# A four-layer scan network on one core: order of the y copy, of the z and C stores, of a job's first loads, and PSUM banks at the end

## The chip, the cores and the metric

The kernel runs on one core of one Trainium2 chip. The metric is the device time of one execution in microseconds. The runs shown are three executions of the kernel before, and one profiled execution, whose trace all views come from.

## What is computed

The input is 4 images of 64 x 64 positions with 96 channels. Four layers follow one another, each a mixer with a residual and a small feed-forward net with a residual. Cut to what matters here, in layers 1 to 3:

```python
# x: (4, 64, 64, 96); layers 1..3
xz = layernorm(x) @ in_proj_w.T                 # 192 channels for x, 192 for z
xc = silu(depthwise_conv3x3(x_part) + conv_b)
# four directions: rows, columns, and both reversed; 16 states
dA = exp(dt * A);  h = dA * h + (dt * u) * B;  y = sum_n h_n * C_n + D * u
y  = sum of the four directions, layernorm, * silu(z), @ out_proj_w.T
x  = x + y
t  = x + W2 @ relu(W1 @ layernorm(x) + b1) + b2     # operands rounded to fp8, sums to fp16
```

Layer 0 has another recurrence (A, B and C are projections of each position, the output is gated), and the same feed-forward net.

## The kernel before, in words

The work is one program, written out in order for each engine: a wrapper (`InOrder`) makes every engine carry out its instructions in the order in which the Python code emits them. All instructions bear the line of that wrapper (L78) in the profile, so the views go by tile names.

**Stages.** `gated` does layer 0 for all images. Then `scans` does 12 stages (layers 1 to 3, four images each). A stage has 24 items: 2 directions, 4 segments of T = 1024 positions, 3 chunks of 128 partitions (64 channels in two orders). An item has NS = 16 steps, one for each state n. So there are 12 x 24 x 16 = 4608 steps k.

**One step k of `scans`**, in the order of emission: ACT copies the end of the last scan (`carry(k - 1)`); SP issues the rows of C for step k + 2, two broadcast loads into one of six tiles `c`, and ACT makes the decays `da` for k + 2 (`c_rows`, `decays`); PE broadcasts B for k + 1 into one of two wide PSUM tiles `bc` (`b_rows`); POOL multiplies the last state row by C (`times_c(k - 1)`, h in three tiles); if step k - 4 was an item's last, `store` copies the sum `acc` from PSUM into `y` on ACT and sends it to HBM with four DMAs; DVE multiplies du by B and scans (`scan(k, beside)`), and between those two `beside` emits side work; PE adds the product of step k - 3 into `acc` (`accumulate`, two PSUM banks, one buffer). The first `accumulate` of an item also puts in D * u or the y of the other direction. `store` of an item is thus emitted at n = 3 of the next one, just before the first `accumulate` of that item, which needs the same `acc`.

**Side work.** Side work is in generators; each `yield` ends a link, and `pump` emits one link. A generator that yields True needs a free bank among two single PSUM banks (`bank`, `release`, `settle`). `prepare_chunk` makes delta and du for the next item, `prepare_segment` projects u to dt, B and C rows of the next segment and sends C to HBM (`cs`), from where `c_rows` broadcasts it. Both get one link a step, and are drained at n = 13.

**Jobs.** `between(im, layer, dst)` is the end of one layer and the start of the next for one image: `first` loads y (two halves of `cols_a` and two of `part_c`, and the first strip's `pad` tiles); then, over 8 strips of 512 positions, three chains side by side: `joins` (y of four directions transposed and added on PE, `y_t`), `mixers` (norm, gate by z, `out_proj`), `feeds` (the feed-forward net). Then `takes` (norm, input projection, z) and `convolves` (3 x 3 convolution, Silu, u and z to HBM). `Job.step` gives its chains `rate` rounds of links a step: 1.65 for the next stage's image, 2.6 for the last ends of images 0 to 2 in the last two stages and for layer 0's. A norm needs a logarithm on ACT; norms wait in `pending`, and `logarithms` serves all at once: at n = 11 of each item, in `prepare_chunk`, or when a job has waited `patience` rounds. The job of the next stage must be done at n = 4 of item 22 of a stage; what is left then is emitted at once.

**The end.** The last image's end runs alone after the scans: `Job(between(images[-1], 3, images[-1].dst), patience=1).finish()`. There logarithms come when no chain can emit a link.

**PSUM.** One pool `pbc` holds the two wide tiles (four banks) and the two single banks; a second pool (`pl0`, then `pac`) holds the sums (two banks).

The lines that the steps are about:

```python
            if 0 <= k - 1 <= last:
                carry(k - 1)
            if k + 2 <= last:
                c_rows(k + 2)
                decays(k + 2)
...
            if k >= 4 and (k - 4) % NS == NS - 1:
                store(items[(k - 4) // NS])
            if k <= last:
                scan(k, beside)
            if 0 <= k - 3 <= last:
                accumulate(k - 3)
            settle()
```

Of the kernel before, what the change touches and what calls it, by code (L numbers as in the profile page):

```python
# [10 lines left out]
F32 = mybir.dt.float32  # L11
# [88 lines left out]
def metaformer(ctx: ExitStack, tc: tile.TileContext, x, l0_ab, l0_rest, ssm, ffn, out):  # L100
# [13 lines left out]
    def const(name, shape, dtype=F32):  # L114
        return pools[1].tile(shape, dtype, name=name)

    def wide():
        return pbc.tile([128, T], F32, tag="bc", name="bc")


    banks = {"free": 2, "back": 0}

    def bank(name):
        banks["free"] -= 1
        return pbc.tile([128, MM], F32, tag="ps", name=name)

    def release():
        banks["back"] += 1

    def settle():  # L130
        banks["free"] += banks["back"]
        banks["back"] = 0
# [423 lines left out]

    def gate_z(im, s, hold):
        if s < NSTRIP:
            t = slice(s * MM, (s + 1) * MM)
            for z, a in zip(hold["z"].pop(s), (0, 128)):  # L560
                act.activation(z, z, AF.Silu)
                sp.dma_start(out=im.z[a : a + z.shape[0], t], in_=z)

    def convolve(im, layer, s, hold):

        lo, hi = hold["pads"].pop(s)
        taps = weights[layer]
        w = taps.w
        raw = []
        groups = (  # L570
            [(taps.lo[:, t, :], lo[:, t // 3 : t // 3 + SR, t % 3 : t % 3 + HW]) for t in range(9)],
            [(taps.hi[:, t, :], hi[:, 0:SR, t : t + HW]) for t in range(3)]
            + [(taps.hi[0:64, 3 + t, :], hi[0:64, 2 : 2 + SR, t : t + HW]) for t in range(3)],
        )
        for i, group in enumerate(groups):
            ps = bank("conv")
            for at, (lhs, rhs) in enumerate(group):
                pe.matmul(ps, lhs, rhs, start=at == 0, stop=at == len(group) - 1)
                yield
            v = sb(1, f"u{i}", [128, MM])  # L580
            act.copy(v, ps)
            release()
            yield i == 0
            raw.append(v)
        for i, v in enumerate(raw):
            act.activation(v, v, AF.Silu, bias=w[:, W_CB + i : W_CB + i + 1])
        gate_z(im, s + 1, hold)
        yield
        yield
        t = slice(s * MM, (s + 1) * MM)  # L590
        cols_a, part_c = hold["cols"]
        sp.dma_start(out=im.u[0, 0:64, t], in_=raw[0][0:64])
        sp.dma_start(out=im.u[1, 0:64, t], in_=raw[0][64:128])
        sp.dma_start(out=im.u[2, 0:64, t], in_=raw[1][0:64])
        for p, src, dst, c0, nc_ in (
            (slice(0, 128), raw[0], cols_a, 0, HW),
            (slice(0, 64), raw[1], part_c, 0, HW // 2),
            (slice(64, 128), raw[1], part_c, HW // 2, HW // 2),
        ):
            pool.tensor_copy(  # L600
                dst[p].rearrange("p (c r) -> p r c", r=HW)[:, SR * s : SR * s + SR, :],
                src[p].rearrange("p (r c) -> p r c", c=HW)[:, :, c0 : c0 + nc_],
            )
            if p.start or p.stop == 128:
                yield
        if s == NSTRIP - 1:
            yield
            sp.dma_start(out=im.u[1, 64:128, :], in_=cols_a[0:64])
            sp.dma_start(out=im.u[0, 64:128, :], in_=cols_a[64:128])
            for k in range(2):  # L610
                sp.dma_start(
                    out=im.u[2, 64:128, k * L // 2 : (k + 1) * L // 2],
                    in_=part_c[64 * k : 64 * k + 64],
                )

    def between(im, layer, dst=None):
# [8 lines left out]
        def first():  # L625
            if layer:
                cols_a, part_c = hold["cols"] = columns()
                sp.dma_start(out=cols_a[0:64], in_=im.y[1, 64:128, :])
                sp.dma_start(out=cols_a[64:128], in_=im.y[0, 64:128, :])
                for k in range(2):  # L630
                    sp.dma_start(
                        out=part_c[64 * k : 64 * k + 64],
                        in_=im.y[2, 64:128, k * L // 2 : (k + 1) * L // 2],
                    )
                load_y(im, 0, hold)
            yield
            yield
            yield

        yield [Chain(first())]  # L640
        done = {"y": 0, "x": 0, "end": 0}
# [55 lines left out]
        def convolves():  # L697
            yield lambda: done["in"] > 0
            gate_z(im, 0, hold)
            for s in range(NSTRIP):  # L700
                yield lambda: done["in"] > min(s + 1, NSTRIP - 1)
                yield True
                yield from convolve(im, layer + 1, s, hold)
                done["out"] += 1
# [3 lines left out]
    class Job:  # L708
# [23 lines left out]
                    logarithms()  # L732
                    self.waited = 0

        def finish(self):
            while not self.done:
                self.step()
                settle()


# [22 lines left out]
    def prepare_segment(item, sg):  # L763

        xp = weights[item.layer].xp
        m = NB3 + 2 * R

        def project(ps, a, b, k):

            for c in range(3):  # L770
                o = (3 * item.d + c) * XPW
                cols = slice(k * MM, (k + 1) * MM)
                pe.matmul(
                    ps[0 : b - a],
                    xp[:, o + a : o + b],
                    sg.us[c][:, cols],
                    start=c == 0,
                    stop=c == 2,
                )
                if c:  # L780
                    yield

        sg.rows = sb(1, "rows", [128, T])
        for k in range(2):
            cols = slice(k * MM, (k + 1) * MM)
            ps = bank("x_proj_b")
            yield from project(ps, 0, m, k)

            bs = sg.bs[:, cols]
            act.copy(sg.rows[NB3:m, cols], ps[NB3:m])  # L790
            sg.steps = k == 1
            act.copy(bs, ps[0:NB3])
            yield
            rem = sg.rows[0:NB3, cols]
            dve.tensor_tensor(rem, ps[0:NB3], bs, ALU.subtract)
            release()
            yield
            for p in (32, 64):
                act.copy(bs[p : p + 32], rem[p : p + 32])
            yield k == 0  # L800
        pool.tensor_tensor(sg.bs[64:96], sg.rows[64:96], sg.bs[64:96], ALU.subtract)
        for k in range(2):
            cols = slice(k * MM, (k + 1) * MM)
            yield True
            ps = bank("x_proj_c")
            yield from project(ps, m, m + NC2, k)
            act.copy(sg.rows[0:NC2, cols], ps[0:NC2])
            release()
        sp.dma_start(out=sg.cs, in_=sg.rows[0:NC2])

    def prepare_chunk(item):
# [48 lines left out]
    def scans(stages, jobs, pac):  # L860
# [94 lines left out]
        def accumulate(k):  # L955
# [7 lines left out]
                    add_quarters(i, i.yf, stacked, True, False)  # L963
            add_quarters(i, h, stacked, False, n == NS - 1)

        def store(i):
            y = sb(2, "y", [128, T])
            act.copy(y, i.acc)
            for j in range(2):
                for k in range(2):  # L970
                    o = 64 * (j ^ k)
                    t = i.seg * T + k * MM
                    sp.dma_start(
                        out=i.im.y[i.chunk, 64 * j : 64 * j + 64, t : t + MM],
                        in_=y[o : o + 64, j * MM : (j + 1) * MM],
                    )

        chain = segment = None
# [15 lines left out]
        for k in range(last + 5):  # L994
# [23 lines left out]
            def beside():  # L1018
# [5 lines left out]
                        drain(segment, work)  # L1024
                work()

            if 0 <= k - 1 <= last:
                carry(k - 1)
            if k + 2 <= last:
# [5 lines left out]
                b_rows(k + 1)  # L1035
            if 0 <= k - 1 <= last:
                times_c(k - 1)
            if k >= 4 and (k - 4) % NS == NS - 1:
                store(items[(k - 4) // NS])
            if k <= last:  # L1040
                scan(k, beside)
            if 0 <= k - 3 <= last:
                accumulate(k - 3)
            settle()
# [241 lines left out]
    for i, im in enumerate(images):  # L1286
        im.src = x[i * L : (i + 1) * L, :]
        im.dst = out[i * L : (i + 1) * L, :]
    with tc.tile_pool(name="pl0", bufs=1, space=bass.MemoryType.PSUM) as pl0:
        gated(images, Job(between(images[0], 0), 2.6, patience=1), pl0)  # L1290
    stages = [(im, layer) for layer in range(1, 4) for im in images]
    jobs = []
    for at in range(len(stages)):
        jobs.append([])
        if at + 1 < len(stages):
            im, layer = stages[at + 1]
            jobs[-1].append(Job(between(im, layer - 1), 1.65))

        for im in {10: images[:2], 11: images[2:3]}.get(at, ()):
            jobs[-1].append(Job(between(im, 3, im.dst), 2.6))  # L1300
    with tc.tile_pool(name="pac", bufs=1, space=bass.MemoryType.PSUM) as pac:
        scans(stages, jobs, pac)
    Job(between(images[-1], 3, images[-1].dst), patience=1).finish()

# [115 lines left out]
```

## Time and profile before

| what | value |
|---|---|
| median of three runs | 19681.59 us (19680.81 to 19689.28) |
| the profiled execution | 19688.32 us, span 19686.5 us |
| layer 0 (`gated`) | 0 to 1817 us |
| scans of 12 stages | 1817 to 19394 us, 4608 steps |
| the last image's end | 19394 to 19687 us |
| mean granted clock of PE | 0.815 |
| a scan, a multiply on DVE | 2343 ns, 1208 ns |
| copy of y on ACT | 288 times, median 993 ns |
| C rows, from issue to landing | median 4.2 us |

In the page and the answers, DVE is VectorE, ACT ScalarE, POOL GpSimd, PE TensorE's matmuls, PEld its weight loads, SP SyncE, which issues the DMAs here. A group line reads: engine, operation, out<-in, shapes, count | busy us, mean ns of one | idle time of the engine just before these instructions, and what ended most of it. A waits line reads: who <- for whom: us in total, times, longest. A timeline line reads: start us, length us, engine, line, operation, tiles, shapes, count, and in brackets the idle time before and what ended it.

### The profile page before, as it was taken

To read this page: it belongs to the slowest core of one execution; us is meant where nothing else is said; L and a number is where in the kernel's file an instruction comes from. 1 tells how busy PE (TensorE), PEld (TensorE's weight loads), DVE (VectorE), ACT (ScalarE), POOL (GpSimd) and SP (SyncE) were. 2 spreads that over 40 slices of the span, in tenths; PEclk is the share of its full clock that TensorE was granted. 3 is DMA by queue.
4 is the path that set the end of the run, shared out by engine and by line. 5 is a ranking of instruction groups with operands and counts; after the bars stand their busy time and mean duration, and the time that the engine had idled before them with its cause. 6 is when DMAs were issued, how large, how long until landed. Compare 5 with 4: busy or idle time off the path is not lost. (4 is left out here: it accounts for less than half of the span.)

```text
span 19686.5 us, 224801 instructions
## 1 busy us (share of the span) xinstructions
PE 16267.7 (83%) x70400; PEld 4750.9 (24%) x70400; DVE 17666.9 (90%) x13768; ACT 12256.8 (62%) x19331; POOL 15495.8 (79%) x10086
## 2 busy tenths in 40 slices
PE   8998787787888887787887888787888888888876
PEld 3332121121122222222222222222222222222223
DVE  6757999999999999999999999999999999998884
ACT  4544665665665665665666666666666666666664
POOL 3435888888888888888888888888888888878884
PEclk9998787787887797797797787797887787787886
DMA  2213676666676667666666676666666666676663
GB/s 52 50 48 87 169 185 168 170 187 164 171 189 173 166 184 182 168 185 178 170 188 176 170 186 172 170 188 174 171 186 172 170 189 174 171 187 169 165 176 89
DMA packets 1269876, 3192.65 MB, mean 162 GB/s; under 512 B 440336, under 2 KB 440560, under 8 KB 1262544
## 3 DMA queue, kind: packets, MB, share of 16 engines
q1 hardware_dynamic: 1268688, 3178.27, 61.5%
q8 instruction: 568, 9.31, 0.2%
q14 instruction: 620, 5.08, 0.1%
HBM read 2818.81 MB, written 308.28 MB: 159 GB/s over the span
## 5 line engine op out<-in xcount | busy, mean ns | idle before, releaser
L78 POOL TENSOR_TENSOR c<-h,c 128x1024 f32<-128x1024 f32 (+1 forms) x4992 | 11334.8, 2277 | 3377.8 <-DVE h L78 1478.0
L78 DVE TENSOR_TENSOR_SCAN h<-da,carry,bc 128x1024 f32<-128x1024 f32 x4608 | 10795.4, 2343 | 530.3 <-POOL c L78 17.0
L78 PE MATMUL acc<-c,twice 64*64 64x512 f32 x36864 | 6215.7, 751 | 20.1 <-POOL c L78 20.0
L78 ACT ACTIVATE da<-delta,decay 128x1024 f32<-128x1024 f32 x4608 | 5280.9, 1147 | 1491.5 <-DVE h L78 1475.6
L78 DVE TENSOR_TENSOR bc<-du,bc 128x1024 f32<-128x1024 f32 x4608 | 5565.6, 1208 | 488.4 <-PE bc L78 461.6
L78 PE MATMUL bc<-bs,sel 96*128 96x512 bf16 x9216 | 3384.4, 455 | 2343.3 <-DVE h L78 2235.9
L78 ACT COPY carry<-h 128x1 f32<-128x1 f32 x3456 | 649.5, 188 | 3374.5 <-DVE h L78 3368.7
L78 PEld LDWEIGHTS <-sel 96*128 96x128 bf16 x9216 | 552.2, 101 | 7301.0 <-DVE h L78 5519.2
L78 PEld LDWEIGHTS acc<-c,twice 64*64 64x64 f32 x36864 | 1130.7, 153 | 2799.4 <-issue 1860.2
L78 ACT ACT_TABLE_LOAD x1155 | 1481.9, 1283 | 36.5 <-DVE mv L78 20.3
L78 PE MATMUL conv<-pad,tap_lo 128*128 128x512 f32 x1728 | 906.5, 634 | 0.0
L78 PE MATMUL dt_proj<-rows,w 12*128 12x512 f32 x1152 | 826.5, 804 | 6.4 <-ACT delta L78 6.4
L78 ACT ACTIVATE du<-e,ones 128x1024 f32<-128x1024 f32 x576 | 659.3, 1145 | 199.3 <-POOL delta L78 194.5
L78 POOL TENSOR_TENSOR delta<-delta,du 128x1024 f32<-128x1024 f32 x288 | 679.8, 2361 | 72.0 <-ACT du L78 70.3
L78 PE MATMUL x_proj_b<-u,xp 128*108 128x512 f32 x1152 | 687.6, 713 | 46.4 <-DMA xp<-in_ssm 15.5
L78 PE MATMUL x_proj_c<-u,xp 128*32 128x512 f32 x1152 | 642.0, 672 | 76.1 <-ACT rows L78 67.0
L78 POOL TENSOR_TENSOR e<-e,du 128x1024 f32<-128x1024 f32 x288 | 679.8, 2360 | 2.4 <-ACT du L78 2.4
L78 ACT ACTIVATE c<-c,l_bias 128x512 f32<-128x512 f32 x384 | 263.6, 686 | 670.5 <-PE c L78 665.9
L78 POOL TENSOR_TENSOR du<-delta,u 128x1024 f32<-128x1024 f32 x288 | 680.4, 2363 | 0.1
L78 POOL TENSOR_TENSOR delta<-delta,e 128x1024 f32<-128x1024 f32 x288 | 678.8, 2357 | 0.1
L78 PE MATMUL conv<-pad,tap_hi 128*128 128x512 f32 (+1 forms) x1152 | 601.8, 624 | 0.6 <-ACT u L78 0.5
L78 DVE TENSOR_TENSOR_SCAN h<-da,l_carry,bc 128x512 f32<-128x512 f32 x384 | 491.4, 1280 | 41.9 <-DVE bc L78 2.3
(152 smaller groups left out, 15200.8 us busy)
## 6 DMA issues: line engine op xcount, KB each, us to landing
c<-cs SPq DMA_DIRECT2D x9216, 256.0 KB, 4.2
u<-u SPq DMA_DIRECT2D x288, 512.0 KB, 6.7
y<-y SPq DMA_DIRECT2D x1152, 128.0 KB, 3.2
y<-y SPq DMA_DIRECT2D x144, 512.0 KB, 6.8
xr<-x SPq DMA_DIRECT2D x224, 192.0 KB, 5.1
u<-u SPq DMA_DIRECT2D x288, 128.0 KB, 3.6
pad<-y SPq DMA_DIRECT2D x288, 128.0 KB, 4.9
z<-zl SPq DMA_DIRECT2D x96, 256.0 KB, 2.0
```

The lines of the kernel that those rows point to most:

```text
L78: ins = f(*a, **k).ins
```

## The change

Four edits, and a regrouping of PSUM pools that the last one needs.

1. `store` is parted. `take` (the copy of `acc` into `y`) is emitted first in the step, ahead of `carry` and `decays`; the four DMAs are emitted after `scan`.
2. The stores of z go into `store_z`, two links after the Silu that makes z. The store of C in `prepare_segment` goes one link after its last copy.
3. `first` yields nine times instead of three when the layer has a scan before it (layer > 0), so that it takes ten links.
4. The wide tiles go into a pool of their own (`pbig`), which is closed with `pac` before the last image's end; that end then takes its banks from a pool of six (`pend`). Its job has rate 3 instead of 1.4, and `finish(eager=True)` calls `logarithms` after each round in which a norm is pending.

```diff
+    wides = []
+
     def wide():
-        return pbc.tile([128, T], F32, tag="bc", name="bc")
+        return wides[0].tile([128, T], F32, tag="bc", name="bc")
...
-    banks = {"free": 2, "back": 0}
+    banks = {"free": 2, "back": 0, "pool": pbc}
     def bank(name):
         banks["free"] -= 1
-        return pbc.tile([128, MM], F32, tag="ps", name=name)
+        return banks["pool"].tile([128, MM], F32, tag="ps", name=name)
...
     def gate_z(im, s, hold):
         if s < NSTRIP:
+            for z in hold["z"][s]:
+                act.activation(z, z, AF.Silu)
+
+    def store_z(im, s, hold):
+        if s < NSTRIP:
             t = slice(s * MM, (s + 1) * MM)
             for z, a in zip(hold["z"].pop(s), (0, 128)):
-                act.activation(z, z, AF.Silu)
                 sp.dma_start(out=im.z[a : a + z.shape[0], t], in_=z)
...
         gate_z(im, s + 1, hold)
         yield
         yield
+        store_z(im, s + 1, hold)
         t = slice(s * MM, (s + 1) * MM)
         cols_a, part_c = hold["cols"]
         sp.dma_start(out=im.u[0, 0:64, t], in_=raw[0][0:64])
...
                 load_y(im, 0, hold)
-            yield
-            yield
-            yield
+            for _ in range(9 if layer else 3):
+                yield
...
             gate_z(im, 0, hold)
+            yield
+            yield
+            store_z(im, 0, hold)
             for s in range(NSTRIP):
...
-        def finish(self):
+        def finish(self, eager=False):
+
             while not self.done:
                 self.step()
+                if eager and pending:
+                    logarithms()
                 settle()
...
             act.copy(sg.rows[0:NC2, cols], ps[0:NC2])
             release()
+        yield
         sp.dma_start(out=sg.cs, in_=sg.rows[0:NC2])
...
+        def take(i):
+            i.y = sb(2, "y", [128, T])
+            act.copy(i.y, i.acc)
+
         def store(i):
-            y = sb(2, "y", [128, T])
-            act.copy(y, i.acc)
             for j in range(2):
                 for k in range(2):
                     o = 64 * (j ^ k)
                     t = i.seg * T + k * MM
                     sp.dma_start(
                         out=i.im.y[i.chunk, 64 * j : 64 * j + 64, t : t + MM],
-                        in_=y[o : o + 64, j * MM : (j + 1) * MM],
+                        in_=i.y[o : o + 64, j * MM : (j + 1) * MM],
                     )
...
+            full = items[(k - 4) // NS] if k >= 4 and (k - 4) % NS == NS - 1 else None
+            if full is not None:
+                take(full)
             if 0 <= k - 1 <= last:
                 carry(k - 1)
...
-            if k >= 4 and (k - 4) % NS == NS - 1:
-                store(items[(k - 4) // NS])
             if k <= last:
                 scan(k, beside)
+            if full is not None:
+                store(full)
...
+    with tc.tile_pool(name="pbig", bufs=2, space=bass.MemoryType.PSUM) as wides_pool:
+        wides.append(wides_pool)
...
-    Job(between(images[-1], 3, images[-1].dst), patience=1).finish()
+    with tc.tile_pool(name="pend", bufs=6, space=bass.MemoryType.PSUM) as pend:
+        banks.update(free=6, back=0, pool=pend)
+        Job(between(images[-1], 3, images[-1].dst), 3, patience=1).finish(eager=True)
```

More of the change, by code (lines that the diff above doesn't have):

```diff
@@ L1288, in metaformer @@
         im.dst = out[i * L : (i + 1) * L, :]
[L1289 to L1302, printed above, removed]
-    Job(between(images[-1], 3, images[-1].dst), patience=1).finish()
+    with tc.tile_pool(name="pbig", bufs=2, space=bass.MemoryType.PSUM) as wides_pool:
+        wides.append(wides_pool)
+        with tc.tile_pool(name="pl0", bufs=1, space=bass.MemoryType.PSUM) as pl0:
+            gated(images, Job(between(images[0], 0), 2.6, patience=1), pl0)
+        stages = [(im, layer) for layer in range(1, 4) for im in images]
+        jobs = []
+        for at in range(len(stages)):
+            jobs.append([])
+            if at + 1 < len(stages):
+                im, layer = stages[at + 1]
+                jobs[-1].append(Job(between(im, layer - 1), 1.65))
+            for im in {10: images[:2], 11: images[2:3]}.get(at, ()):
+                jobs[-1].append(Job(between(im, 3, im.dst), 2.6))
+        with tc.tile_pool(name="pac", bufs=1, space=bass.MemoryType.PSUM) as pac:
+            scans(stages, jobs, pac)
+    with tc.tile_pool(name="pend", bufs=6, space=bass.MemoryType.PSUM) as pend:
+        banks.update(free=6, back=0, pool=pend)
+        Job(between(images[-1], 3, images[-1].dst), 3, patience=1).finish(eager=True)
 def _layer0(W_in, b_in, W_out, b_out, gamma, beta):
```

## The prediction

> **What bounds the kernel now.** I read the busy shares first, then busy times by stretch, then the table of waits, then the timeline around the places that the change touches.
>
> ```profile
> PE 16267.7 (83%) x70400; PEld 4750.9 (24%) x70400; DVE 17666.9 (90%) x13768; ACT 12256.8 (62%) x19331; POOL 15495.8 (79%) x10086
> L78 DVE TENSOR_TENSOR_SCAN h<-da,carry,bc 128x1024 f32<-128x1024 f32 x4608 | 10795.4, 2343 | 530.3 <-POOL c L78 17.0
> L78 DVE TENSOR_TENSOR bc<-du,bc 128x1024 f32<-128x1024 f32 x4608 | 5565.6, 1208 | 488.4 <-PE bc L78 461.6
> ```
>
> VectorE (DVE) is the bound. 4608 steps of one multiply (1208 ns) and one scan (2343 ns) make 16.4 of the 19.7 ms; the only large wait is for the broadcast of B by TensorE (PE), 461.6 us. The next view gives busy time in the scan stages, in the first joins of the last image's end, and in that whole end (columns: window, length, then PE, PEld, DVE, ACT, POOL busy, granted clock, DMA share, GB/s).
>
> ```profile
> 1817.00:19394.00 17577.00, 14493.68 (x65366) 4019.14 (x65366) 16465.77 (x11920) 11330.46 (x17389) 14733.86 (x8758) 0.81 0.67 176
> 19421.00:19442.00 21.00, 19.20 (x128) 12.85 (x128) 3.04 (x16) 2.60 (x8) 0.00 (x0) 0.50 0.46 104
> 19394.00:19687.00 293.00, 176.47 (x864) 109.15 (x864) 30.22 (x144) 104.03 (x227) 67.02 (x137) 0.50 0.19 45
> ```
>
> DVE idles 17577 - 16466 = 1111 us in the scans[...]. So all four edits together fight over some 600 us in the scans and over the 293 us tail, in which no engine is full.
>
> ```profile
> DVE bc L78 <- PE bc L78: 461.6, 271, 20.7
> POOL c L78 <- DMA c<-cs: 285.7, 78, 14.0
> ACT y L78 <- PE acc L78: 164.4, 87, 13.9
> PE acc L78 <- ACT y L78: 163.7, 154, 2.9
> PE y_t L78 <- DMA pad<-y: 116.5, 12, 23.3
> SPq L78 <- ACT zl L78: 332.5, 96, 27.7
> ```
>
> Columns: total, times, longest. The copy of y holds PE for 163.7 us, and PE holds that copy for as long. A job's first loads hold PE 12 times, one of them in the tail. The z stores hold the queue of SyncE (SP) for 332.5 us.
>
> [...] C rows land in 4.2 us by the page's median, yet POOL waits 10 to 14 us for one behind a job's first loads. [...] 19.2 of 21 us busy, clock still 0.50. I count on no faster clock there.
>
> **Step 1, y first on ACT (288 copies of 993 ns).** Now the copy stands behind carry (188 ns) and decays (1147 ns), both of which wait for the last scan; in the new order it stands ahead of them. Two copies as they are now:
>
> ```profile
> 10489.10 0.99 ACT L78 COPY y<-acc 128x1024 f32<-128x1024 f32 x1
> 10490.15 1.09 PE L78 MATMUL acc<-u,skipd 64*64 64x512 f32 x8 [1.56 <-ACT y L78]
> ...
> 12015.09 1.01 ACT L78 COPY y<-acc 128x1024 f32<-128x1024 f32 x1 [1.45 <-PE acc L78]
> ```
>
> In the first, PE waits for the copy, and an earlier copy helps. In the second the copy waits for PE, and nothing is won. Over 287 copies in the timeline (the last has no next chunk) I took the time at which the sum is complete, A, against the end of the scan that carry waits for, E. A is before E in 89; there the copy could start sooner, all cases together 213 us. Capped by PE's wait after the same copy that is 126 us, and capped again by DVE's wait for B in the three steps after it, 29 us (46 without PE's cap). I take 35 us won. In the other 198 A is after E. Now carry and decays run while PE finishes; in the new order they wait too, so ACT ends the step later by A - E, at most 0.19 + 1.15 = 1.34 us: 194 ACT-us in all. Queued behind are decays, the delta activations that free PE's banks, and the job's copies. Decays of step k+2 have cover: they are due at E + 2 x 3.60 + 1.25 = 8.45 us and would end at A + 2.3; A - E is 4.1 us at the ninth decile and 6.8 at most. The rest reaches DVE through PE only in part; the trace doesn't show the share. Between 0 and 194 us I take a tenth, 20 us, since ACT is busy 64% of this stretch. Net -15 us, bounds -46 and +148. The four y stores go to SP after the scan's helpers instead of before; nobody reads them soon, so zero.
>
> **Step 2, z and C sent behind their data.** 96 pairs of z stores go two links later, 96 C stores one link. I looked behind every z wait over 4 us in the scans: in the 15 us after it no POOL wait for C rows follows. C rows are issued two steps ahead into six buffers, which is the cover; the longest hold there is 6.4 us. In layer 0 the next strip's x load does come late (DVE waits of 5 us in seven strips), but the u stores ahead of it need Silu results that are ready only half a microsecond sooner, and they stay ahead. So 0 us; at best about 7 x 5 = 35 us. The extra link of C is drained before the next chunk needs it. Loss: a job gets 8 links more (six of step 3), 8/1.65 x 3.6 = 17 us later; jobs end at least 8 steps (29 us) ahead of the forced drain, so zero.
>
> **Step 3, ten links for first loads.** Six links more: at 1.65 a step 6/1.65 x 3.60 = 13.1 us later for y_t on PE, at 2.6 a step 8.3 us. Eleven jobs in the scans load y (columns: start, length):
>
> ```profile
> 10499.72 0.77 PE L78 MATMUL y_t<-ident,pad 128*128 128x128 f32 x2 [5.87 <-DMA pad<-y]
> 10502.07 4.67 POOL L78 TENSOR_TENSOR c<-h,c 128x1024 f32<-128x1024 f32 x2 [11.67 <-DMA c<-cs]
> 10505.04 1.23 DVE L78 TENSOR_TENSOR bc<-du,bc 128x1024 f32<-128x1024 f32 x1 [6.31 <-PE bc L78]
> ```
>
> Eight look like this, with PE waits of 3.8 to 6.2 us, so 13.1 us removes them, and DVE waits of 6.0, 5.0, 5.7, 6.3, 4.7, 5.1, 5.4 and 5.4 = 43.6 us. **But POOL is late next.** Its C row still lands where it does, and h has three buffers, so the third scan after must wait for POOL. A place without any y_t shows that wait alone:
>
> ```profile
> 2918.10 2.34 POOL L78 TENSOR_TENSOR c<-h,c 128x1024 f32<-128x1024 f32 x1 [8.81 <-DMA c<-cs]
> 2920.47 2.35 DVE L78 TENSOR_TENSOR_SCAN h<-da,carry,bc 128x1024 f32<-128x1024 f32 x1 [1.76 <-POOL c L78]
> ```
>
> For the example: scan at 10489.18 + 3 x 3.604 = 10499.99, POOL done at 10502.07 + 2.35 = 10504.42, so 4.4 us stay. Over the eight this way 27.5 us stay, and with 0.5 us of disturbance each 31.5: 12 us won. The other three run at 2.6 a step, with PE waits of 23.3, 13.4 and 15.6 us and DVE waits of 20.7, 11.3 and 14.4. Here 8.3 us go from each, 25 us; the rest stays. Step 3: -37 us, bounds -12 and -60.
>
> **Step 4, the tail on six banks.** 27 us until the first pads land, then PE works 174.8 us in 266, 21.8 us a strip, and the chain shows out_proj returning every 60 us for two strips. Logarithms come only when all chains stand still, so feeds, mixers and joins go in convoys. With eager logarithms and banks for each, they overlap, and PE's 21.8 us a strip are the floor. Each norm costs two table loads of 1.28 us (ten loads now, up to 32 after: 28 us more on ACT, under PE). I take 25 us a strip: 27 + 16 (first join 11, logarithm to refinement 5) + 8 x 25 + 22 (last feed) = 265, so -28 us. At 22 a strip -52, at 29 it is +4. PSUM pools and their changeover: nothing, one wait for finished work.
>
> **Sum.** -15 + 0 - 37 - 28 = -80 us. The profiled execution took 19688.3 us (span 19686.5, 1.8 around it); it becomes 19608. It lies 6.7 us over the median of the runs, so I forecast 19681.6 - 80 = **19602 us**, 0.41% less. A difference under 0.2% (39 us) can't be told from no change.
>
> **Rivals.** *The covers are thin* (chance 0.17): 46 us at the copies, 58 at the loads, 52 in the tail, 156 us in all, 19526. For it: PE waits for y in 154 places. Against: POOL's wait stands behind the loads. *The next wait takes over* (0.16): nothing net at the copies, 12 us at the loads since POOL and PE still wait, 10 in the tail: -22, 19660. For it: POOL waits 285.7 us for C rows, which no edit removes. *ACT's head of line* (0.12), the slower side: the copy at the queue's head waits for PE in 198 places, and all 194 us come through to DVE. -35 + 194 - 37 - 28 = +94, 19776. It decides against the change from 51% of the 194 us on (100 us undone), by over 0.2% from 72%. For it: ACT releases the banks that PE needs at n = 4 and 5, where DVE's steps run over 3.60 us by 80 and 116 us in all, more than at any other n. Against it: PE, late by itself, leaves ACT idle time there.
>
> **Chances.** The forecast case (-40 to -125) has 0.55. Faster by over 0.2%: 0.55 + 0.17 = 0.72; within: 0.16; slower: 0.12. The range goes from 19530 to 19672; it leaves out the slower rival and the far end of the first, under 0.2.
>
> **What would show it.** PE's wait for ACT's y falls below 60 us and ACT's wait for PE's sum rises; the DVE waits at the eight first loads shrink to 3 to 5 us with POOL's C as releaser; PE's wait for pads is left in the tail and the three late jobs; POOL's 286 us for C rows stay; the tail is 240 to 280 us with 20 to 32 table loads. I am wrong if DVE's waits for PE grow after the copies, or if the later jobs meet the u loads at new places and the scans lose there what the loads gave.

## The result, and the profile after

The changed kernel took 19613.61 us in the median of six runs (19604.67 to 19656.49), the kernel before 19682.17 us in runs on the same chip: a ratio of 0.9968 with a 95% interval of 0.9957 to 0.9978, or -63 us (-85 to -43). The forecast of 19602 us lies 12 us below it. The profiled execution took 19605.71 us, with a span of 19603.9 us. The total came out as forecast. Two of its four parts did not, and the experiments are about that.

The page's two groups of DVE, which are to be held against the first block of the prediction:

```profile
L78 DVE TENSOR_TENSOR_SCAN h<-da,carry,bc 128x1024 f32<-128x1024 f32 x4608 | 10797.5, 2343 | 598.7 <-POOL c L78 80.8
L78 DVE TENSOR_TENSOR bc<-du,bc 128x1024 f32<-128x1024 f32 x4608 | 5567.1, 1208 | 417.8 <-PE bc L78 389.6
```

Busy times are within 2 us of those of before, means the same. DVE's idle time ahead of the multiplies fell from 488.4 to 417.8 us, that ahead of the scans rose from 530.3 to 598.7 us, and POOL's C is now named for 80.8 us where it was 17.0. One wait has taken the place of another. Busy times in the scans and in the last image's end:

```profile
1804.00:19388.00 17584.00, 14533.33 (x65366) 4017.53 (x65366) 16467.88 (x11919) 11313.07 (x17391) 14733.80 (x8758) 0.81 0.67 175
19388.00:19604.00 216.00, 162.97 (x864) 108.75 (x864) 29.75 (x144) 113.57 (x235) 67.51 (x137) 0.51 0.26 61
```

The scans took 17584 us, no less than the 17577 us of before. The end fell from 293 to 216 us. The waits:

```profile
ACT y L78 <- PE acc L78: 708.9, 246, 14.2
DVE bc L78 <- PE bc L78: 389.6, 271, 5.1
POOL c L78 <- DMA c<-cs: 295.3, 80, 13.6
DVE h L78 <- POOL c L78: 81.5, 37, 12.5
PE y_t L78 <- DMA pad<-y: 42.2, 4, 23.2
PE acc L78 <- ACT y L78: 35.4, 69, 2.1
```

PE's wait for the copy fell from 163.7 to 35.4 us. The copy's own wait for PE rose from 164.4 to 708.9 us: ACT now stands with the copy at its head, in 246 places where it was 87. POOL's wait for C rows is about what it was (285.7 before).

A job's first loads, at the place that the prediction shows:

```profile
10508.51 4.65 POOL L78 TENSOR_TENSOR c<-h,c 128x1024 f32<-128x1024 f32 x2 [10.51 <-DMA c<-cs]
10510.89 2.35 DVE L78 TENSOR_TENSOR_SCAN h<-da,carry,bc 128x1024 f32<-128x1024 f32 x1 [3.46 <-POOL c L78]
10514.12 0.63 PE L78 MATMUL y_t<-ident,pad 128*128 128x128 f32 x2
```

PE no longer waits for y. DVE waits 3.46 us for POOL, where it waited 6.31 us for PE.

**How far one profile can be read.** Eight kernels of this study (the one before and seven experiments) have the same layer 0. In their profiles it took 1799 to 1817 us. Four of them (the one before and three with only the end changed) have the same scans too, and these took 17567 to 17603 us. So differences under some 40 us between single profiles of the scans are not read below. Totals come from medians with intervals. Places are read by their step n: the cells of the table further down agree within 8 us among these four profiles.

### The profile page after: what moved, and what is told of

Same layout as the page of the kernel before. It is cut to its first block, busy times and chain, and to the rows that moved or that the text cites. A ratio compares the mean times of both kernels' runs of the same rounds, so it can differ in the third digit from the quotient of the medians.

```text
span 19603.9 us, 224830 instructions
## 1 busy us (share of the span) xinstructions
PE 16279.3 (83%) x70400; PEld 4745.4 (24%) x70400; DVE 17669.3 (90%) x13768; ACT 12248.8 (62%) x19341; POOL 15496.4 (79%) x10086
## 5 line engine op out<-in xcount | busy, mean ns | idle before, releaser
L78 DVE TENSOR_TENSOR_SCAN h<-da,carry,bc 128x1024 f32<-128x1024 f32 x4608 | 10797.5, 2343 | 598.7 <-POOL c L78 80.8
L78 DVE TENSOR_TENSOR bc<-du,bc 128x1024 f32<-128x1024 f32 x4608 | 5567.1, 1208 | 417.8 <-PE bc L78 389.6
L78 ACT COPY y<-acc 128x1024 f32<-128x1024 f32 x288 | 291.3, 1012 | 713.8 <-PE acc L78 708.9
```

Source lines behind the costliest of these rows:

```text
L78: ins = f(*a, **k).ins
```

## The experiments

All ratios are against the kernel before, run on the same chip, in three groups of four kernels. Its medians there were 19675.5, 19669.3 and 19675.7 us. A us figure is (ratio - 1) x 19675.

### The four parts alone

Each kernel has one of the four edits whole; of each diff the deciding lines are repeated.

y copied first in ACT's step, stores after the scan (step 1):

```diff
+            if full is not None:
+                take(full)
             if 0 <= k - 1 <= last:
                 carry(k - 1)
...
                 scan(k, beside)
+            if full is not None:
+                store(full)
```

> Step 1 alone: the kernel before with the copy of y first in the step, its stores after the scan. The changed kernel's scans took 7.5 us longer than before although the first loads gave back 41 us there, so some 49 us were lost elsewhere in the scans. Theory A (the copy at the head of ACT's queue costs what the loads give): scans 20 to 50 us longer than 17576.5, total +20 to +50, stages 0 to 2 alone about +15; layer 0 and the tail unchanged. Theory B (the jobs' links, shifted by the other steps, collide at new places; the copy is harmless): scans within 15 us of before or shorter by up to 35, total -35 to +15. The forecast had -15.

z and C sent later (step 2):

```diff
         yield
         yield
+        store_z(im, s + 1, hold)
...
+        yield
         sp.dma_start(out=sg.cs, in_=sg.rows[0:NC2])
```

> Step 2 alone: z stores two links and the C store one link later. Layer 0 gave 13.4 us in the changed kernel and only this step reaches it: both theories expect layer 0 at about 1804 us. Theory A (the copy costs): scans as before within 10 us, total about -13. Theory B (shifted links collide): scans 20 to 50 us longer, total +5 to +35. The forecast had 0.

Ten links for the first loads (step 3):

```diff
-            yield
-            yield
-            yield
+            for _ in range(9 if layer else 3):
+                yield
```

> Step 3 alone: ten links for a job's first loads. Both theories: DVE's losses at the eight first loads of stages 3 to 10 fall from about 5.6 to 3.5 us each with POOL's product with C as releaser, and the three late ones fall by 8 us each, -41 us together. Theory A (the copy costs): the rest of the scans within 10 us, total -35 to -45. Theory B (shifted links collide): a part is lost again, total -20 to +5. Layer 0 and the tail unchanged.

Six banks, rate 3 and eager logarithms at the end (step 4):

```diff
-    Job(between(images[-1], 3, images[-1].dst), patience=1).finish()
+    with tc.tile_pool(name="pend", bufs=6, space=bass.MemoryType.PSUM) as pend:
+        banks.update(free=6, back=0, pool=pend)
+        Job(between(images[-1], 3, images[-1].dst), 3, patience=1).finish(eager=True)
```

> Step 4 alone: the last image's end on six banks, rate 3, eager logarithms. Layer 0 and the scans are instruction for instruction those of before, so 1817 and 17576 us within 5 us also show how far two profiles of one program differ. The tail should be 216 us as in the changed kernel, 77 us less than 293; total -70 to -80. If the tail's gain needs the other steps, it would stay above 240 us.

| part alone | ratio, interval | us | forecast |
|---|---|---|---|
| step 1 | 1.0048 (1.0036 to 1.0060) | +94 | -15 |
| step 2 | 0.9999 (0.9991 to 1.0007) | -2 | 0 |
| step 3 | 0.9979 (0.9970 to 0.9988) | -41 | -37 |
| step 4 | 0.9961 (0.9949 to 0.9973) | -77 | -28 |

Two forecasts held and two did not, with opposite signs. The sum of the parts is -26 us and the whole is -63. The five intervals together allow a difference of some 46 us, so these 37 us alone don't show that the parts act on each other; steps 1 and 2 are run together below.

The expectations ahead of these runs held for steps 3 and 4. The +94 us of step 1 lie beyond both of its theories (+50 at most), and step 2's interval (-18 to +14 us) doesn't part its two. The scans of the kernel with step 4 alone took 26 us longer than those of before, not the same within 5 us.

### What of step 1 costs: the copy or the stores

The copy first, the stores where they were:

```diff
+            if full is not None:
+                take(full)
             if 0 <= k - 1 <= last:
                 carry(k - 1)
...
+            if full is not None:
+                store(full)
             if k <= last:
                 scan(k, beside)
```

> The copy of y first in ACT's step, the four y stores left where they were, ahead of the scan. Theory H (the copy at the head of ACT's queue holds carry, decays and the delta activations): the loss of step 1 alone stays whole, +60 to +95 us against the kernel before. Theory S (the moved y stores fall behind a waiting z store on SP and take C rows and u loads with them): 0 to +30 us.

It took 1.0036 (1.0024 to 1.0049), +71 us: most of the loss of step 1 is the copy's. The copy where it was, the stores after the scan:

```diff
+            if full is not None:
+                take(full)
             if k <= last:
                 scan(k, beside)
+            if full is not None:
+                store(full)
```

> The copy of y at its old place, behind carry and decays; only the four y stores are emitted after the scan. Theory H: within 15 us of the kernel before. Theory S: +40 to +80 us, since the order of SP's queue is that of step 1.

It took 1.0009 (1.0001 to 1.0017), +18 us: just over what the first theory allowed and far under what the second asked. Both mechanisms exist, and the copy's is the larger. Steps 1 and 2 together, their two diffs in one kernel:

> Steps 1 and 2 together, without the ten links and the six banks. Theory S: a z store sent two links later no longer holds SP ahead of the y stores, so step 1's +95 us shrink to about +45 us. Theory H: step 2 doesn't touch ACT's order, so +90 to +100 us stay.

It took 1.0028 (1.0019 to 1.0038), +55 us. Step 2 does nothing alone and takes about 40 us (9 to 69 by the intervals) off step 1. The stores' 18 us lie within what the two intervals allow. With it the parts add up: 55 - 41 - 77 = -63 us, which is the whole.

**Where it happens.** From each trace I took the end of every scan less the end of the one before, less 3.604 us, and added up this excess over all 12 stages by chunk and step n. Cells in us:

| kernel | 3rd chunk, n=5 | 3rd chunk, n=7 | 3rd chunk, n=8, 9 | 2nd chunk, n=9 | 1st chunk, n=7 |
|---|---|---|---|---|---|
| before | 62 | 7 | 42 | 16 | 46 |
| stores moved alone | 57 | 8 | 38 | **41** | 43 |
| copy first alone | 43 | **55** | 62 | 16 | 57 |
| step 1 | 44 | **51** | 65 | **40** | 55 |
| steps 1 and 2 | 41 | **53** | 69 | 14 | 56 |
| the change | 42 | **48** | 52 | 13 | 28 |

The stores make one cell, the copy makes another, and step 2 removes that of the stores. The gain that step 1 was made for is there too, at n = 5 of the third chunk: 18 us. With the copy first alone the five cells rise by 60 us together, which is the whole rise of the excess in the scans (57 us): 48 at n = 7, 20 at n = 8 and 9, and 11 in the first chunk, less the gain. Only the cell at n = 7 was followed further.

**The stores' cell.** SP's queue in the kernel before, and with the stores moved, at the same place of the program (SPq lines: start, time of issue):

```profile
8560.76 2.38 SPq L78 DMA_DIRECT2D y<-y  x4
8565.09 0.33 SPq L78 DMA_DIRECT2D z<-zl  x1
8567.39 3.54 SPq L78 DMA_DIRECT2D u<-u  x6
```

```profile
8565.42 0.33 SPq L78 DMA_DIRECT2D z<-zl  x1
8566.45 2.51 SPq L78 DMA_DIRECT2D y<-y  x4
8570.28 4.51 SPq L78 DMA_DIRECT2D u<-u  x6
8577.01 3.72 PE L78 MATMUL x_proj_b<-u,xp 128*108 128x512 f32 x4 [3.24 <-DMA u<-u]
8584.53 1.23 DVE L78 TENSOR_TENSOR bc<-du,bc 128x1024 f32<-128x1024 f32 x1 [3.63 <-PE bc L78]
```

Before, SP issues the y stores at 8560.76, in the time in which it would only wait for z, and z at 8565.09. Moved, they come behind z: SP issues nothing for 4.83 us ahead of z at 8565.42, and the y stores only from 8566.45 on. The 2.51 us of their issue delay the u loads of the next segment, which start 4.86 us after z where it was 2.30. PE waits 3.24 us for u, and the broadcast of B that stands behind on PE comes 3.63 us late for DVE. With z sent later too, the trace has the y stores at 8550.01, three u loads at 8553.81 and z only at 8555.44: the y stores and these loads go ahead of z, and the cell is back at 14 us.

**The copy's cell.** Stage 8, item 17, before and with the copy first alone. The scan of n = 3 starts at 14458.99 in the first and at 14470.21 in the second, so 11.22 us are to be taken off the second for a comparison:

```profile
14461.92 1.01 ACT L78 COPY y<-acc 128x1024 f32<-128x1024 f32 x1 [0.87 <-PE acc L78]
14468.53 0.56 ACT L78 COPY rows<-x_proj_c 32x512 f32<-32x512 f32 x1
14469.14 1.90 PE L78 MATMUL x_proj_c<-u,xp 128*32 128x512 f32 x4 [0.96 <-ACT rows L78]
14470.98 1.12 PE L78 MATMUL z<-hq,w 96*128 96x512 f32 x2
14472.03 1.09 PE L78 MATMUL acc<-c,twice 64*64 64x512 f32 x8
14473.06 0.61 PE L78 MATMUL bc<-bs,sel 96*128 96x512 bf16 x2
14473.70 1.23 DVE L78 TENSOR_TENSOR bc<-du,bc 128x1024 f32<-128x1024 f32 x1 [0.37 <-PE bc L78]
```

```profile
14473.12 1.01 ACT L78 COPY y<-acc 128x1024 f32<-128x1024 f32 x1 [2.00 <-PE acc L78]
14480.87 0.56 ACT L78 COPY rows<-x_proj_c 32x512 f32<-32x512 f32 x1
14481.48 2.33 PE L78 MATMUL x_proj_c<-u,xp 128*32 128x512 f32 x4 [2.09 <-ACT rows L78]
14483.74 2.08 PE L78 MATMUL z<-hq,w 96*128 96x512 f32 x2
14485.75 1.99 PE L78 MATMUL acc<-c,twice 64*64 64x512 f32 x8
14487.67 1.03 PE L78 MATMUL bc<-bs,sel 96*128 96x512 bf16 x2
14488.74 1.23 DVE L78 TENSOR_TENSOR bc<-du,bc 128x1024 f32<-128x1024 f32 x1 [4.20 <-PE bc L78]
```

The copy starts no sooner (2.93 and 2.91 us after that scan began), because PE's sum isn't there. ACT waits 2.00 us at it instead of 0.87, so what stands behind it comes later. That is 1.13 us, and it goes down ACT's queue whole: the copy of the projected rows comes 1.12 us later. PE waits for the rows, since they hold a bank, and 1.13 us longer. But DVE waits 3.83 us longer. The rest goes with PE's clock. Busy times of this stretch in the second kernel, and of the like stretch in the first (the clock is the third number from the end):

```profile
14483.50:14488.70 5.20, 5.20 (x14) 1.01 (x14) 1.04 (x1) 5.16 (x7) 4.52 (x2) 0.50 0.00 2
```

```profile
14469.00:14474.00 5.00, 4.86 (x17) 1.11 (x18) 4.50 (x4) 4.96 (x10) 4.92 (x3) 1.00 0.54 135
```

In the second kernel the clock stood at 0.50 from 14482.82 us on, 1.3 us after the gap of 2.09 us; in the first, after the gap of 0.96 us, it stayed full. The four groups of matmuls up to the broadcast of B took 0.43, 0.96, 0.90 and 0.42 us longer for it. These 2.71 us and the 1.13 make the 3.83 us.

The changed kernel has the same delay at the same place of the program:

```profile
14461.52 1.01 ACT L78 COPY y<-acc 128x1024 f32<-128x1024 f32 x1 [2.01 <-PE acc L78]
14469.88 1.90 PE L78 MATMUL x_proj_c<-u,xp 128*32 128x512 f32 x4 [2.09 <-ACT rows L78]
14474.43 1.23 DVE L78 TENSOR_TENSOR bc<-du,bc 128x1024 f32<-128x1024 f32 x1 [1.49 <-PE bc L78]
```

PE's gap is 2.09 us here too, but its clock stays full, and DVE waits 1.49 us, which is the delay and no more. So the length of the gap alone doesn't decide. In the clock records of these traces the clock is 0.50 or 1.00 and changes only on a grid of 3.413 us. With the copy first alone 61% of one period of that grid falls into the gap; in the changed kernel the gap is split, 9% of one period and 52% of the next. I counted the periods at full clock in the scans of the kernel before. Of 503 in which PE was busy for less than half, 494 were followed by a period at half clock; of the 2679 others, 134. The period of the first gap, with PE busy for 39%, is like those 494. The changed kernel's second period, with 48%, is not: in that kernel's scans 323 of the 328 periods at full clock with PE busy for 40 to 50% were followed by half clock, and this is one of the other five. The count doesn't explain that place.

With the copy first alone there are 19 such places at n = 7, with DVE waits of over 1 us and 43 us in all. In 8 of them, with 22 us of the wait, the sum's matmuls ran slow, as in the place above (1.99 us for eight instead of 1.09). In the other 11 they did not, and in seven of these DVE waited 1.49 to 1.50 us, the plain delay. The part of the clock is read from such places and counts; no experiment set the gap by itself.

### Is that place all of it?

The changed kernel, with the copy back at its old place in the third chunk's items, the ones beside which rows are projected:

```diff
-            if full is not None:
+            early = full is not None and q % 3 != 2
+            if early:
                 take(full)
...
+            if full is not None and not early:
+                take(full)
             if k <= last:
                 scan(k, beside)
```

> The changed kernel, but in the items of the third chunk, beside which the next segment is projected, the copy of y stays behind carry and decays; its stores still go after the scan. Theory P (the place: an ACT held by the copy makes the copies of the projected rows late there, and PE and the broadcast of B behind them): the 44 us of DVE excess at n = 7 of the third chunk fall to about 5, and the kernel takes about -105 to -130 us against the kernel before, as the change without its first part. Theory E (the copy costs everywhere that PE's sum is late): -60 to -85 us, as the changed kernel.

And the change without step 1 (its other three diffs in one kernel; `store` is whole and at its old place):

> The change without its first part: z and C sent later, ten links, six banks at the end, and the copy of y where it was. If step 1 costs in the whole change what is left of it after the interaction (about 45 us), this is -105 to -120 us against the kernel before, some 19560 us, and faster than the changed kernel. If step 1 is harmless once z is sent later, it is -60 to -85 us, as the changed kernel.

The first took 0.9936 (0.9924 to 0.9949), -126 us, the second 0.9935 (0.9923 to 0.9948), -128 us, which is better than either of its theories had it. As far as intervals of 25 us to either side tell, the third chunk's copies thus carry the whole cost of step 1. In the first kernel the cell at n = 7 is back at 7 us (and the gain at n = 5 is gone, 60). In the other two chunks, a copy first in the step is worth nothing that can be measured, and the copies' waits for PE, still 495 us in all, cost nothing that shows. Without step 1 the change would have been worth twice as much.

### The end: banks or logarithms

Six banks and rate 3, without eager logarithms; then eager logarithms and rate 3 on two banks:

```diff
-        Job(between(images[-1], 3, images[-1].dst), 3, patience=1).finish(eager=True)
+        Job(between(images[-1], 3, images[-1].dst), 3, patience=1).finish(eager=False)
```

> Only the tail is changed: six banks and rate 3, but logarithms come only when no chain can emit a link, as in the kernel before. Theory L (logarithms, not banks, make the convoys): 0 to -20 us, the tail stays at 270 to 290 us. Theory B (banks make them): -50 to -77 us.

```diff
-    with tc.tile_pool(name="pend", bufs=6, space=bass.MemoryType.PSUM) as pend:
-        banks.update(free=6, back=0, pool=pend)
+    with tc.tile_pool(name="pend", bufs=2, space=bass.MemoryType.PSUM) as pend:
+        banks.update(free=2, back=0, pool=pend)
```

> Only the tail is changed: eager logarithms and rate 3, with two banks as in the kernel before. Theory L: most of the 77 us, -50 to -77 us, and a tail of 215 to 240 us. Theory B: 0 to -25 us, since every join, mixer and feed must wait for a free bank.

Banks without eager logarithms: 0.9999 (0.9991 to 1.0007), nothing. Eager logarithms with two banks: 0.9967 (0.9955 to 0.9980), -65 us. Their ends, in this order:

```profile
19372.00:19660.00 288.00, 171.71 (x868) 107.86 (x864) 30.58 (x145) 103.94 (x227) 66.96 (x137) 0.51 0.19 46
```

```profile
19379.00:19612.00 233.00, 167.44 (x864) 109.85 (x864) 29.67 (x144) 116.05 (x237) 66.98 (x137) 0.51 0.24 57
```

The late logarithm made the convoy. Banks give 5 us at most while it holds (293 to 288) and some 17 us (233 to 216) once it is gone; an unchanged end repeats within 1 us in six profiles (292.1 to 293.1). Rate 3 is in both kernels, so eager logarithms at the old rate of 1.4 were not tried.

### What is left at the first loads

The change without step 1, with the 3 MB of a job's first loads in eight pieces:

```diff
-                sp.dma_start(out=cols_a[0:64], in_=im.y[1, 64:128, :])
-                sp.dma_start(out=cols_a[64:128], in_=im.y[0, 64:128, :])
...
+                for p in range(8):
+                    h = p % 2
+                    if p < 4:
+                        t = slice(h * L // 2, (h + 1) * L // 2)
+                        to = cols_a[64 * (p // 2) : 64 * (p // 2) + 64, t]
+                        sp.dma_start(out=to, in_=im.y[1 - p // 2, 64:128, t])
...
+                    yield
+                    yield
                 load_y(im, 0, hold)
-            for _ in range(9 if layer else 3):
+            for _ in range(4 if layer else 3):
                 yield
```

> The change without its first part, and a job's first loads in eight pieces, one every second link, with four links after them (20 links in all). Theory Q (what is left at the first loads is POOL's wait for C rows queued behind 3 MB of loads): the DVE excess of about 29 us at the eight first loads falls under 8 us and that of the three late jobs by half, so about -160 us against the kernel before (-145 to -180). Theory K (the job's later links fall on new places and lose what the loads give): -110 to -140 us, though the excess at the first loads is gone.

It took 0.9909 (0.9894 to 0.9924), -179 us, the fastest kernel of the study at 19500.93 us. POOL waits 206.2 us for C rows instead of 307.6 us. One of the two largest losses that the edit brought:

```profile
7464.08 3.72 PE L78 MATMUL x_proj_b<-u,xp 128*108 128x512 f32 x4 [18.98 <-DMA xp<-in_ssm]
7469.85 1.23 DVE L78 TENSOR_TENSOR bc<-du,bc 128x1024 f32<-128x1024 f32 x1 [17.95 <-PE bc L78]
```

At the eight first loads of stages 3 to 10, 0.7 us of excess are left in all, of 29 us without the pieces. So what was left there was POOL's wait for C rows behind bulk loads, as far as this run tells: the excess went when the loads came in pieces. The three late jobs gained nothing: 45 us of excess in the 20 steps from their first loads, with and without the pieces, where half was expected to go.

The edit also loses. In two stages the job, now 10 links longer, is not done at n = 4 of item 22, when it is due: its last convolution ends 5 us after that step's scan begins, and 54 us before it without the pieces. What is left of it is emitted at once. On SP the last load that the next projection needs (`xp`) is issued behind the job's late stores, PE waits 18.98 us for it at the place shown, and the excess is 18.1 and 19.4 us. The last image's end took 238 us instead of 216, since there nobody needs the pieces. A rate a little above 1.65 and undivided loads in the end might give back some of these 59 us; that was not tried.

The 51 us between this kernel and the one without pieces are therefore not the loads alone: the loads gave 28 us, and the edit lost these 59. By the two profiles some 65 us more were gained elsewhere in the scans, where the job's links now meet other steps. Cells moved both ways: at n = 9 of the first chunk the excess fell from 73 to 37 us and at n = 5 of the third from 58 to 30, while at n = 7 and n = 12 of the third it rose from 7 to 24 and from 18 to 37. No run parts these shifts from the pieces.

## Why the prediction was right in total and wrong in parts

**Step 1 failed, by 70 us.** The forecast was -15 us, and what the step did within the change is +55 (steps 1 and 2 together). Three of its terms failed. *"I take 35 us won"*: about 18 are seen won, at n = 5 of the third chunk. *"I take a tenth, 20 us"*, of the 194 us that ACT loses: with the copy first alone the net loss is 71 us, which with the 18 won makes 89 of 194, or 46%. I had spread a loss evenly over ACT's idle time. It was not even: at the place followed it fell where PE waits for ACT's next copy, came through whole (1.12 us), and DVE's wait grew with PE's half clock to 3.83 us; in 8 of the 19 places the matmuls ran slow. The prediction had named this as a sign of being wrong, that DVE's waits for PE grow after the copies. *"Nobody reads them soon, so zero"* of the y stores: who reads them was the wrong question. What counted was what stood behind them on SP, which was C rows and u loads, for +18 us alone. The rival of ACT's head of line had the right mechanism. It named 51% as the point from which it decides, and the copy came to 46%. It pointed to the wrong steps, though: the excess at n = 5 fell, and most of the loss is at n = 7, the rest at n = 8 and 9 and in the first chunk.

**Step 2 was right alone** (0 forecast, -2 measured) and incomplete in company: its delay of z undoes the stores' loss of step 1. I had costed the two edits one by one against the old order of SP.

**Step 3 was right, mechanism and size**: -41 us for -37. At the eight loads DVE's excess went from 44.5 to 28.0 us, so 16.5 went where 12 were forecast, with POOL's C as the releaser that was named. PE's waits for pads fell from 116.5 to 42.2 us, 23.2 of that in the end, as forecast. POOL's 286 us for C rows stayed, as forecast.

**Step 4 was right in kind and mis-sized by 49 us**, -77 for -28. The term that failed is the 25 us a strip. The chain of the changed kernel returns every 20.1 us:

```profile
19506.94 6.01 PE y_t L78 x37
19527.05 6.00 PE y_t L78 x38
```

That is below what I had called the floor, 21.8 us, which was PE's busy time of the old end over eight. The busy time itself fell, from 176 to 163 us, so it was no floor; why it fell is open, and the ends of matmuls in the profile are modelled. Eight strips save 39 us, and beginning and end together take 55 us instead of 65. The end was forecast at 240 to 280 us and took 216. Table loads, 1.28 us each, came to 18, just under the 20 to 32 forecast. The pool changeover cost nothing visible: PE waits 23.24 us for the first pads of the end, and waited 23.06 before.

**The sum.** Of the 1111 us that DVE idled in the scans before, 488 us are 3756 gaps of under 150 ns, 133 ns in the median; the other 622 us are what the edits could fight over there. -80 forecast; +70 from step 1 (with step 2), -49 from step 4 and -4 from step 3 make -63, as measured. Two errors of 50 to 70 us nearly cancelled, and to that extent the forecast time was luck.

## What to carry to other kernels

Moving an instruction ahead in its engine's order of work helps only where its input is ready by then (here in 89 of 287 places, by the trace of before); count the places where it is not, and follow each delay to the next engine that waits for a result from there (1.13 us on ACT here, 3.83 us on DVE), instead of taking a share of idle time for a cover. Price a moved DMA by what is issued behind its new place (+18 us here for the stores alone), and price edits of one engine's order together (steps 1 and 2 here: +55 us, where the parts alone had +94 and -2). Where several small chains stand still for one shared event (a batched logarithm here), free the event before giving them more buffers: here the banks alone were worth nothing that could be measured.

## What the hardware showed that I had not expected

PE's clock fell within the work of one step, and the length of the gap ahead did not decide it. A gap of 2.09 us was followed by 6.83 us at 0.50 in one kernel, and DVE waited 4.20 us. In another kernel the same gap at the same place lay otherwise on the grid of 3.413 us, the clock stayed full, and DVE waited 1.49 us. In the scans of the kernel before, periods at full clock with PE busy for less than half were followed by half clock in 494 of 503 cases. That the gap's place on the grid made the difference is my reading of these two places; no run here moved a gap alone.

The clock also stayed down under dense work: in the middle of the changed kernel's end PE is busy 58.85 of 60 us, and the clock is still 0.50.

```profile
19507.00:19567.00 60.00, 58.85 (x321) 40.92 (x320) 11.32 (x57) 41.17 (x88) 24.52 (x51) 0.50 0.19 47
```

The stretch is longer and denser than the one before the change, where the share was 19.2 of 21 us at the same clock. The middle of the end is now full of PE's work at half its clock. The busy share doesn't decide this: of the periods of 3.413 us at half clock in which PE was busy for 97% or more, 570 of 918 were followed by full clock in the changed kernel's scans, and 1 of 37 in its end. Nor is it a fault of the clock record: the `ff_y` matmuls start 80 ns after one another in the end, as they do at half clock in the scans, and 43 ns at full clock there. What sets the matmuls of the end apart is open, and no run here tells; 736 of the 864 are in fp32 and 64 to 128 columns wide, with means of 318 to 478 ns.
